# Differential attention and a Hadamard FFN on one core: the third input block transposed by VectorE through DRAM, FFN weights in 256-byte runs, transform levels in other steps

## The chip, the core and the metric

The kernel runs on one NeuronCore of a Trainium2 chip. The core has a matrix engine (TensorE, PE in the profile; PEld is its weight load), VectorE (DVE), ScalarE (ACT), GpSimd (POOL), an engine that only issues transfers (SyncE, SP), and 16 DMA engines. Data lie in SBUF (128 partitions), in PSUM (the accumulators that TensorE writes) and in DRAM. Each engine works through its own instructions in order and waits at semaphores for the others. The metric is the device time of one execution in microseconds (us), lower is better.

## The reference

The input x has 2048 tokens of 256 numbers, all in float32. Two layers follow, each with its residual:

```python
x = x + _layernorm(attention(_layernorm(x)))
x = x + _layernorm(ffn(_layernorm(x)))

# attention: 8 pairs of query heads (D = 128), 4 groups of key/value pairs
p = softmax(q1 @ k1.T) - lam * softmax(q2 @ k2.T)    # causal, 2048 x 2048 for each pair
o = p @ v                                             # v is 256 wide
o = o * rsqrt(mean(o * o) + EPS) * subln_w * (1.0 - LAMBDA_INIT)
return o @ out_w.T + out_b

# ffn: fwht is the normalised Walsh-Hadamard transform over the last dimension
x = fwht(x * SU_ug) / SCALE
x = silu(x @ W_gate.T * s_gate) * (x @ W_up.T * s_up)
x = fwht(x * SU_dp) / SCALE
x = x @ W_down.T * s_down
```

## The kernel before, in words

**Units and steps.** The attention of a group g (4 groups) is cut into units. `Unit(g, i, subs)` stands for row block i of 128 tokens: the first eight blocks are one unit each (both halves of 64 rows, "short"), the last eight two units (one half each, "long"). A program written out by hand runs one step per unit: in step s the scores and exponentials of unit s, the combination of the two softmaxes of unit s-1 (`combine`, L332 for the factor `cf` and L337 for the sum) with its transposition (`turn`, L360, and the way through DRAM, L362 and L372), and `values` (L388) of unit s-3. `inverse` on GpSimd (L415 to L418) and `turn_out` (L434) bring a finished block's output to `project_out` (L455). Group 0 has steps 0 to 23, group 1 has steps 24 to 47, with the long units first. The table of `put` calls adds other work to a step: ahead of it (`before`), behind the first half of its scores (`mid`, `between`) or at its end (`after`). An engine's order of instructions is the order in which this program is written.

**The scores.** A unit's two score products go to PSUM tiles of 1024 columns, of which three rotate (`ps_s`, shared with the projections). VectorE empties them (L279, and L290 for the last 64 columns under the mask) into `e` and finds the minimum; ScalarE takes exponentials in place (L305).

**A transposition without TensorE.** VectorE's stream transpose turns each 32x32 block of a tile. The tile is then stored to DRAM and loaded back by four transfers, one for each band of 32 partitions, which puts the blocks in their places. With pairs of rows laid beside each other the runs are 64 numbers (256 bytes), else 32 (128 bytes).

**The input.** x comes in four blocks of 512 tokens (`xt`, three buffers of a pool `xin`). Each is normalised (`norm_in`, L88 to L103) and transposed to `xnT`, from which queries, keys (`project_heads`, L176, emptied by L195 on ScalarE and L197 on VectorE) and values (`project_values`, L205, emptied by L212) are computed. Block 0 is transposed in halves by TensorE (L503), blocks 1 and 2 by TensorE (`turn_in`, L517, two copies L518 on ScalarE and VectorE), block 3 by VectorE and DRAM (`turn_by_dram`: L523, store L525, four loads L529), with a buffer `xw` of its own.

**The FFN weights.** The transforms are folded into the weights while attention runs. For each of up, gate and down, `load_weights` (L581, a DMA issued by GpSimd) brings 128 x 2048 numbers to a buffer `t0`; down is scaled on ScalarE (L589); `transform` (L612) does one level of the transform with eight GpSimd instructions of 128x256, alternating between the buffers `t0` and `t1`: 8 levels for up and gate, 10 for down. `turn_weights` (L629, four VectorE transposes; L632, one store) puts them to DRAM. Much later, in the last group, `arrive_weights` (L644, four loads for each matrix, issued by SyncE) brings them back in runs of 128 bytes.

**The steps of this work.** The tuple beside "up", "gate" and "down" in the `put` table names a step for each level; loading is at the end of `begin_at`, and the four weight transposes follow the last level by one to three steps (one `after`, one `mid`, one `after`, one `mid`). GpSimd meets the levels of a step behind that step's `inverse` and `pad` (L324, zeros behind the last column). In step 29 it also issues the load of the output weights of group 1 (`load_wo`, L149), which must wait until TensorE has used those of group 0.

Of the kernel before, what the change touches and what calls it, by code (L numbers as in the profile page):

```python
# [10 lines left out]
F32 = mybir.dt.float32  # L11
# [5 lines left out]
P = 128  # L17
# [10 lines left out]
NFC = INTER // P  # L28
# [20 lines left out]
def kernel(  # L49
# [14 lines left out]
    nc = tc.nc  # L64
# [48 lines left out]
    with ExitStack() as actx:  # L113
# [5 lines left out]
        dram = actx.enter_context(tc.tile_pool(name="dram", bufs=4, space=bass.MemoryType.DRAM))  # L119
# [349 lines left out]
        xin = pstack.enter_context(tc.tile_pool(name="xin", bufs=3, side="right"))  # L469
        xsm = pstack.enter_context(tc.tile_pool(name="xsm", bufs=2, side="right"))  # L470
        xts = []
        for b in range(NB):
            xt = xin.tile([P, 4, HID], F32, tag="xt", name=f"xt_{b}")
# [45 lines left out]

        def turn_by_dram(b):  # L520

            xw = xin.tile([P, 2 * 512], F32, tag="xw", name=f"xw_{b}", bufs=1)
            nc.vector.transpose(xw.rearrange("p (c t f) -> p t c f", c=2, t=4), xts[b].rearrange("p t (c f) -> p t c f", c=2))  # L523
            dr = dram.tile([8, 4, 32, 4, 32], F32, tag="dx", name=f"dx_{b}", bufs=2)
            nc.sync.dma_start(  # L525
                dr.rearrange("g b k a w -> (b k) g (a w)"), xw.rearrange("p (g w) -> p g w", g=8)
            )
            for a in range(4):
                nc.sync.dma_start(  # L529
                    xnT[ts(a, 32), b].rearrange("k c (n w) -> k (c n) w", w=32),  # L530
                    dr[:, :, :, a, :].rearrange("g b k w -> k (g b) w"),
                )
# [37 lines left out]
        ffn = {}  # L570
# [7 lines left out]
        def load_weights(which):  # L578
            w = {"up": wup, "gate": wgate, "down": wdown}[which]
            ffn["mixed"] = ffn["tmp"].tile([P, 2 * INTER], F32, tag="t0", name=f"raw_{which}")  # L580
            nc.gpsimd.dma_start(  # L581
                ffn["mixed"].rearrange("p (c f) -> p c f", f=w.shape[1]),
                w.rearrange("(c p) f -> p c f", p=P),
            )

        def scale_down():
# [27 lines left out]

        def turn_weights(which, part):

            w = ffn["mixed"]
            if part == 0:
                ffn["turned"] = ffn["tmp"].tile([P, 2 * INTER], F32, tag="t1", name=f"x_{which}")
            xw = ffn["turned"]  # L620

            order = "p (c f w) -> p f c w"
            src = w.rearrange(order, c=2, f=NFC) if which == "down" else w.rearrange(order, c=NFC, f=2)
            dst = xw.rearrange("p (f c w) -> p f c w", f=src.shape[1], c=src.shape[2])
            if which == "down":
                cut = lambda v: v[:, ts(part, 2)]
            else:
                cut = lambda v: v[:, :, ts(part, 2)]
            nc.vector.transpose(cut(dst), cut(src))  # L629
            if part == 3:  # L630
                ffn["dr", which] = dram.tile([16, 4, 32, 4, 32], F32, tag="dw", name=f"dw_{which}")
                nc.sync.dma_start(  # L632
                    ffn["dr", which].rearrange("g b k a w -> (b k) g (a w)"),
                    xw.rearrange("p (g w) -> p g w", g=16),
                )

        def room_for_weights():
# [4 lines left out]

        def arrive_weights(which, a):
            nc.sync.dma_start(  # L644
                ffn[which][ts(a, 32)].rearrange("k (n w) -> k n w", w=32),
                ffn["dr", which][:, :, :, a, :].rearrange("g b k w -> k (g b) w"),
            )

# [164 lines left out]
        before, mid, between, after = {}, {}, {}, {}  # L813

        def put(where, step, f, *args, **kw):
            where.setdefault(step, []).append(lambda: f(*args, **kw))
# [20 lines left out]
        put(before, 0, project_heads, 0, 1, 1, both=False, n=256)  # L837
        put(mid, 0, turn_in, 1)
        put(mid, 0, norm_in, 2)
        put(mid, 0, project_heads, 0, 1, 2, both=False, n=256)  # L840
        put(mid, 0, project_values, 0, 1)
        put(mid, 0, project_heads, 0, 1, 1, both=True)
        put(mid, 0, lambdas)
        put(between, 0, project_heads, 0, 1, 2, both=False)
        put(before, 1, turn_in, 2)
        put(mid, 1, norm_in, 3)
        put(mid, 1, project_heads, 0, 1, 0, both=True)
        put(mid, 1, turn_by_dram, 3)
        put(mid, 1, project_heads, 0, 2, 0, both=False)
        put(mid, 1, project_heads, 0, 2, 2, both=True)  # L850
# [33 lines left out]
        put(after, 5, open_fold)  # L884
        for which, begin_at, steps in (
            ("up", 5, range(7, 15)),
            ("gate", 17, range(18, 26)),
            ("down", 28, (29, 30, 31, 32, 33, 33, 34, 35, 36, 37)),
        ):
            put(after, begin_at, load_weights, which)  # L890
            if which == "down":
                put(after, begin_at + 1, scale_down)
            for n, step in enumerate(steps):
                put(after, step, transform, which, n)
            for part in range(4):
                put((after, mid)[part % 2], steps[-1] + 1 + (part + 1) // 2, turn_weights, which, part)
        put(after, 40, lambda: ffn["tmp_stack"].close())
        put(after, first + 2, room_for_weights)
        for j, which in enumerate(("up", "gate", "down")):
            for a in range(4):  # L900
                put(after, first + 2 + 4 * j + a, arrive_weights, which, a)
            put(after, first + 6 + 4 * j, sign_weights, which)
# [22 lines left out]
        for step in range(len(units) + LAG + 4):  # L925
            for f in before.get(step, ()):
                f()
            new, mixed = at(step), at(step - 1)
# [104 lines left out]
```

## Time and profile before

| | us |
|---|---|
| median of 3 runs | 1442.96 |
| lowest and highest of them | 1442.91, 1444.27 |
| the profiled execution's own time | 1442.67 |
| its span, first to last instruction | 1440.9 |
| TensorE busy | 1431.5 |
| VectorE busy | 1039.4 |
| ScalarE busy | 508.3 |
| GpSimd busy | 358.7 |

The profile records one execution. Its page gives the busy time of each engine, the span in 40 slices, the DMA queues, the chain of work that ended last and the costliest groups of instructions. Other views of the same trace give the waits of one engine (what it waited for, us in total, times, longest) and a timeline (start in us, duration in us, engine, line, operation, output and input, shape, count; in square brackets the idle time just before and what ended it). Neighbouring instructions of one kind are merged in the timeline. The ends of matmuls are modelled and overlap the next start, so gaps of TensorE are counted from start to start. In a row such as `wup<-dw_up SPq DMA_DIRECT2D x4, 256.0 KB, 7.2` the last number is the median time from the issue of a transfer to its landing.

### The profile page before, as it was taken

How to read it: one execution, taken by the hardware profiler on the slowest of the kernel's cores; microseconds unless marked ns; L12 is line 12 of the kernel's file. 1: busy time of each engine (PE TensorE's matmuls, PEld its weight loads, DVE VectorE, ACT ScalarE, POOL GpSimd, SP SyncE). 2: the span in 40 equal slices, each digit the busy share in tenths (PEclk: the TensorE clock that was granted, in tenths of full speed). 3: DMA queues.
4: the chain of work that ended last, by engine and by line, in shares of the span. 5: the costliest groups of instructions: out<-in, count | busy, mean ns of one | idle time of the engine just before them, and what ended most of it. 6: DMA issues, size and time to landing. Idle time of an engine off the chain costs nothing.

```text
span 1440.9 us, 17707 instructions
## 1 busy us (share of the span) xinstructions
PE 1431.5 (99%) x5444; PEld 1038.5 (72%) x5444; DVE 1039.4 (72%) x2453; ACT 508.3 (35%) x1115; POOL 358.7 (25%) x683
## 2 busy tenths in 40 slices
PE   9999999999999999999999999999999999999998
PEld 7567767656766776776677776675777777888887
DVE  6588897847666888644868779545877799766774
ACT  3453433323123334333433334323424445531111
POOL 2037724632007851011111111111111121121110
PEclk9999999999999999999999999999999999999999
DMA  3379889956487788832788887731999999732110
GB/s 118 73 169 197 198 181 208 191 88 139 94 186 153 163 185 196 166 85 66 153 186 177 173 202 162 134 81 52 206 204 192 192 193 191 166 96 81 52 52 22
DMA packets 511725, 209.75 MB, mean 146 GB/s; under 512 B 404144, under 2 KB 509616, under 8 KB 511632
## 3 DMA queue, kind: packets, MB, share of 16 engines
q1 hardware_dynamic: 508016, 199.42, 66.0%
q0 software_dynamic: 2480, 8.26, 2.2%
q10 hardware_dynamic: 1136, 0.95, 0.2%
q8 instruction: 44, 0.72, 0.2%
q14 instruction: 49, 0.40, 0.1%
HBM read 110.52 MB, written 98.04 MB: 145 GB/s over the span
## 4 chain that ended last, share of the span: by engine, by line
PE 96%; DVE 2%; DMA 1%; issue 0%; POOL 0%; SPq 0%; ACT 0%; POOLq 0%; DVEq 0%
PE po L388 32%; PE sc L264 31%; PE pp L176 11%; PE gu L713 8%; PE pout L455 8%; PE pd L748 4%; PE pv L205 4%; DMA dr<-e 0%; DMA vb<-in_vbias 0%; DVE e L279 0%; PE warm L488 0%; DMA pt<-dr 0%; DVE e L337 0%; DVE e L360 0%; DVE cf L332 0%
## 5 line engine op out<-in xcount | busy, mean ns | idle before, releaser
L388 PE MATMUL po<-v,pt 128*128 128x256 f32 x2176 | 488.2, 379 | 0.4 <-DMA pt<-dr 0.4
L264 PE MATMUL sc<-k,q 128*128 128x512 f32 (+7 forms) x1280 | 478.6, 519 | 2.0 <-DVE last L290 0.9
L388 PEld LDWEIGHTS po<-v,pt 128*128 128x128 f32 x2176 | 425.6, 196 | 60.3 <-issue 11.2
L264 PEld LDWEIGHTS sc<-k,q 128*128 128x128 f32 x1280 | 237.6, 190 | 215.2 <-issue 182.3
L305 ACT ACTIVATE e<-e,last 128x192 f32<-128x192 f32 (+28 forms) x256 | 299.6, 1171 | 223.9 <-DVE last L290 206.2
L279 DVE TENSOR_SCALAR_CACHE_REDUCE e<-sc 128x1024 f32<-128x1024 f32 (+15 forms) x248 | 231.1, 932 | 171.0 <-PE sc L264 169.7
L401 ACT COPY osb<-po 128x256 f32<-128x256 f32 (+1 forms) x96 | 42.5, 443 | 463.7 <-PE po L388 463.7
L415 POOL TENSOR_TENSOR u<-ss,ed 128x1 f32<-128x1 f32 (+1 forms) x96 | 18.3, 191 | 749.4 <-ACT po L404 749.2
L337 DVE SCALAR_TENSOR_TENSOR e<-e,cf,e 128x64 f32<-128x64 f32 (+31 forms) x128 | 173.5, 1376 | 3.4
L360 DVE STREAM_TRANSPOSE e<-e 128x768 f32<-128x768 f32 (+7 forms) x192 | 172.4, 937 | 4.8
L176 PE MATMUL pp<-xnT,wq 128*128 128x512 f32 (+1 forms) x408 | 170.6, 568 | 0.2 <-DVE xnT L504 0.2
L176 PEld LDWEIGHTS pp<-xnT,wq 128*128 128x128 f32 x408 | 77.0, 190 | 78.3 <-issue 74.8
L455 PE MATMUL pout<-wo,oT 128*128 128x256 f32 x512 | 121.0, 379 | 0.0
L279 DVE TENSOR_SCALAR_CACHE_REDUCE e<-sc,mx 128x320 f32<-128x320 f32 (+13 forms) x128 | 97.2, 759 | 21.6 <-PE sc L264 7.8
L455 PEld LDWEIGHTS pout<-wo,oT 128*128 128x128 f32 x512 | 97.2, 190 | 13.1 <-issue 0.3
L290 DVE CUSTOM_DVE_ANT_0 e<-sc,mask,mx 128x64 f32<-128x64 f32 x248 | 70.4, 284 | 8.9
L726 ACT ACTIVATE hT<-gu,colv 128x256 f32<-128x256 f32 x64 | 26.8, 470 | 120.5 <-PE gu L713 120.5
L713 PE MATMUL gu<-fxnT,wgate 128*128 128x256 f32 x256 | 65.8, 379 | 0.0
L713 PE MATMUL gu<-fxnT,wup 128*128 128x256 f32 x256 | 65.7, 379 | 0.0
L418 POOL TENSOR_SCALAR osb<-osb,f 128x256 f32<-128x256 f32 x128 | 61.3, 479 | 12.4
L416 POOL TENSOR_TENSOR f<-u,mhalf 128x1 f32<-128x1 f32 (+1 forms) x96 | 58.4, 608 | 7.5
L732 DVE SCALAR_TENSOR_TENSOR hT<-gu,colv,hT 128x256 f32<-128x256 f32 x64 | 30.6, 478 | 40.5 <-ACT hT L726 40.5
(101 smaller groups left out, 1107.1 us busy)
## 6 DMA issues: line engine op xcount, KB each, us to landing
dr<-e SPq DMA_DIRECT2D x20, 1024.0 KB, 4.7
pt<-dr SPq DMA_DIRECT2D x80, 256.0 KB, 5.7
dr<-e SPq DMA_DIRECT2D x20, 896.0 KB, 4.4
pt<-dr SPq DMA_DIRECT2D x80, 224.0 KB, 5.1
do<-xo SPq DMA_DIRECT2D x64, 256.0 KB, 4.0
oT<-do SPq DMA_DIRECT2D x256, 64.0 KB, 2.6
dr<-e SPq DMA_DIRECT2D x20, 768.0 KB, 4.5
pt<-dr SPq DMA_DIRECT2D x80, 192.0 KB, 4.4
```

Of the source, the lines that this page charges most:

```text
L176: nc.tensor.matmul(pp[:, 512 * h : 512 * h + n], lhsT=wq[:, c, ts(j, P)], rhs=xnT[:, xb, c, lo : lo + n], start=(c == 0), stop=(c == 1),)
L264: nc.tensor.matmul(sc[:, 512 * k : 512 * k + ww], lhsT=qT[m][:, u.i, u.subs[a]].rearrange("d p q -> d (p q)"), rhs=kT[m][:, at + lo : at + ...
L279: nc.vector.tensor_scalar(dst, src, 1.0, best, ALU.mult, ALU.min, accum_out=u.mx[:, k0, c : c + 1],)
L290: nc.vector.tensor_tensor_reduce(e[:, L - 64 : L], sc[:, tail : tail + 64], mask, 1.0, best, ALU.add, ALU.min, accum_out=u.last[:, k0 : k0 ...
L305: nc.scalar.activation(e, e, AF.Exp, bias=u.last[:, 2 * a + m : 2 * a + m + 1], scale=-1.0, accum_out=u.d[:, a, m : m + 1],)
L337: nc.vector.scalar_tensor_tensor(e0, e1, cf[:, a : a + 1], e0, ALU.mult, ALU.add)
L360: nc.vector.transpose(xv[:, r], ev[:, r])
L388: nc.tensor.matmul(u.po[:, ts(a, HID)], lhsT=ptv[:, g, r, :], rhs=vt[:, kc, :], start=(kc == 0), stop=(kc == u.i),)
L416: nc.gpsimd.tensor_tensor(f[:, : u.ns], w[:, : u.ns], mhalf[:, : u.ns], ALU.pow)
L418: nc.gpsimd.tensor_scalar(u.osb[:, a, :], u.osb[:, a, :], f[:, a : a + 1], 16.0, ALU.mult, ALU.mult)
L455: nc.tensor.matmul(u.pout[:, :HID], lhsT=u.oT[:, c, p, :], rhs=wos[u.g][:, p, c, :], start=(p == 0 and c == 0), stop=(p == 1 and c == 1),)
L713: nc.tensor.matmul(ps[:, ts(2 * j + n, 256)], lhsT=ffn[which][:, c, ts(fc, P)], rhs=xnT[:, c, :], start=(c == 0), stop=(c == 1),)
```

## The change

Three things are changed.

1. Block 2 of the input goes the way of block 3. `turn_in(2)`, ahead of step 1, is removed, and `turn_by_dram(2)` stands behind `norm_in(2)` in step 0. The buffers `xw` are no longer a place of their own but take the next of the three buffers of `xt`.
2. The FFN weights are loaded with pairs of rows beside each other (up and gate in four groups of two rows for each partition, down in one), so that the transposed weights are stored in DRAM with runs of 64 numbers, and arrive in runs of 256 bytes instead of 128. The scales of down are laid out to match.
3. The levels take other steps. Gate: 18 to 21, then two each in 22 and 23 (before: one each in 18 to 25). Down: loaded after step 26 (before: 28), levels in 28, 29, 29, 30, 30 and 31 to 35 (before: 29 to 32, 33, 33, 34 to 37). Their transposes and stores move with them, by two steps. Up stays.

```diff
         def turn_by_dram(b):
 
-            xw = xin.tile([P, 2 * 512], F32, tag="xw", name=f"xw_{b}", bufs=1)
+            xw = xin.tile([P, 2 * 512], F32, tag="xt", name=f"xw_{b}")
...
             nc.gpsimd.dma_start(
-                ffn["mixed"].rearrange("p (c f) -> p c f", f=w.shape[1]),
-                w.rearrange("(c p) f -> p c f", p=P),
+                ffn["mixed"].rearrange("p (g c) -> p g c", c=2 * w.shape[1]),
+                w.rearrange("(g p r) f -> p g (r f)", p=P, r=2),
             )
...
-            xw = ffn["turned"]
-
-            order = "p (c f w) -> p f c w"
-            src = w.rearrange(order, c=2, f=NFC) if which == "down" else w.rearrange(order, c=NFC, f=2)
-            dst = xw.rearrange("p (f c w) -> p f c w", f=src.shape[1], c=src.shape[2])
+
+            n, g = (NFC, 1) if which == "down" else (2, 4)
+            src = w.rearrange("p (g r n c) -> p r n g c", g=g, r=2, n=n)
+            dst = ffn["turned"].rearrange("p (n g c r) -> p r n g c", n=n, g=g, r=2)
+            r, half = part % 2, part // 2
             if which == "down":
-                cut = lambda v: v[:, ts(part, 2)]
+                dst, src = dst[:, r, ts(half, 4), 0, :], src[:, r, ts(half, 4), 0, :]
             else:
-                cut = lambda v: v[:, :, ts(part, 2)]
-            nc.vector.transpose(cut(dst), cut(src))
+                dst, src = dst[:, r, half], src[:, r, half]
+            nc.vector.transpose(dst, src)
             if part == 3:
-                ffn["dr", which] = dram.tile([16, 4, 32, 4, 32], F32, tag="dw", name=f"dw_{which}")
+                ffn["dr", which] = dram.tile([8, 4, 32, 4, 64], F32, tag="dw", name=f"dw_{which}")
                 nc.sync.dma_start(
                     ffn["dr", which].rearrange("g b k a w -> (b k) g (a w)"),
-                    xw.rearrange("p (g w) -> p g w", g=16),
+                    ffn["turned"].rearrange("p (g w) -> p g w", g=8),
                 )
...
             nc.sync.dma_start(
-                ffn[which][ts(a, 32)].rearrange("k (n w) -> k n w", w=32),
+                ffn[which][ts(a, 32)].rearrange("k (n w) -> k n w", w=64),
...
         put(mid, 0, norm_in, 2)
+        put(mid, 0, turn_by_dram, 2)
...
-        put(before, 1, turn_in, 2)
...
-            ("gate", 17, range(18, 26)),
-            ("down", 28, (29, 30, 31, 32, 33, 33, 34, 35, 36, 37)),
+            ("gate", 17, (18, 19, 20, 21, 22, 22, 23, 23)),
+            ("down", 26, (28, 29, 29, 30, 30, 31, 32, 33, 34, 35)),
...
-                    a[ff + "Wscale_dp"],
-                )
-            ],
+                )
+            ]
+            + [a[ff + "Wscale_dp"].reshape(P, 2)],
```

## The prediction, made before the result was known

> **What bounds the kernel now.** I read the page first, for its busy line and the chain of work that ended last:
>
> ```profile
> PE 1431.5 (99%) x5444; PEld 1038.5 (72%) x5444; DVE 1039.4 (72%) x2453; ACT 508.3 (35%) x1115; POOL 358.7 (25%) x683
> ...
> PE 96%; DVE 2%; DMA 1%; issue 0%; POOL 0%; SPq 0%; ACT 0%; POOLq 0%; DVEq 0%
> ```
>
> TensorE (PE) is busy for all but 9.4 us of 1440.9, and the granted clock is 9 or more in every slice. So a change that leaves the matmuls alone can win only what PE loses in gaps; the last 5 us and the first 20 hold most of those and are not touched. Next, the waits of PE alone (us in total, times, longest):
>
> ```profile
> PE warm L488 <- POOL ident masks.py:199: 1.5, 1, 1.5
> PE sc L264 <- DVE last L290: 0.9, 2, 0.7
> PE sc L264 <- DVE e L279: 0.7, 1, 0.7
> PE po L388 <- DMA pt<-dr: 0.4, 1, 0.4
> ```
>
> The first is the start. PE's timeline puts the others near 520, 1168 and 1209 us:
>
> ```profile
> 517.94 1.88 PE L264 MATMUL sc<-k,q 128*128 128x512 f32 x4
> 520.54 0.70 PE L264 MATMUL sc<-k,q 128*128 128x256 f32 x2 [0.73 <-DVE e L279]
> 521.44 2.39 PE L264 MATMUL sc<-k,q 128*128 128x512 f32 x6 [0.20 <-DVE last L290]
> ...
> 1168.61 2.40 PE L388 MATMUL po<-v,pt 128*128 128x256 f32 x10 [0.40 <-DMA pt<-dr]
> ```
>
> Matmuls overlap, so the loss is counted in starts. Pieces of 512 columns start 0.43 apart (3.43 for 8). Without a gap the two 256-wide pieces start at 517.94 + 4 x 0.43 = 519.66 and the next at 520.09; it starts at 521.44: **1.35 lost**. At 1168 the six pieces from 1166.11 take 2.10, less 0.16 overlap: 1168.05 instead of 1168.61, **0.56 lost**. At 1209, 0.74 is lost with VectorE (DVE) busy nearly throughout; nothing in the change touches it.
>
> Why is DVE late at 520? Its timeline, and GpSimd's (POOL):
>
> ```profile
> 513.72 2.05 DVE L332 SCALAR_TENSOR_TENSOR cf<-d,nlam,r 128x1 f32<-128x1 f32 x1
> 515.80 1.69 DVE L337 SCALAR_TENSOR_TENSOR e<-e,cf,e 128x1408 f32<-128x1408 f32 x1
> ```
> ```profile
> 510.24 5.51 POOL L612 TENSOR_TENSOR t_down<-t_down 128x256 f32<-128x256 f32 x8
> ```
>
> L332 writes one number per row and has a median of 0.22 us; here it takes 2.05 and ends at 515.77, when POOL's level ends (515.75). The same happens at 161.54: 1.97 us, ending within 0.03 us of a level. Other L332 beside a level take 0.23 to 0.77. The stall at 520 is this 1.83 us too much on DVE.
>
> The Trainium skill, "SBUF — State Buffer", section "SBUF: two separate sides", says a VectorE instruction with two SBUF inputs and a GpSimd one that reads SBUF exclude each other for a whole instruction. The trace agrees in kind; in length, 2.05 us is about three of POOL's 0.69 us instructions. Its rule speaks against packing levels (second rival).
>
> **The change, part by part.**
>
> *Third block.* Eight PE transposes (0.87 us in the chain), an ACT copy (0.57) and a DVE copy (0.69) go. Do the 0.87 come back? The waits in the two built programs say: the first score product of step 1 (sc_1_0_0) waits for L290 of sc_0_0_2 on DVE; the second (sc_1_0_1) for the second L195 that empties pp_1_2_512 on ACT; neither depends on the transposes.
>
> ```profile
> 31.85 0.61 PE L264 MATMUL sc<-k,q 128*128 128x128 f32 x4
> 32.29 1.04 PE L517 MATMUL pst<-ident,xt 128*128 128x128 f32 x8
> 33.17 0.82 PE L264 MATMUL sc<-k,q 128*128 128x192 f32 x4
> ```
> ```profile
> 32.05 1.26 ACT L195 ACTIVATE k<-pp,colv 128x512 f32<-128x512 f32 x2 [0.87 <-PE pp L176]
> ```
>
> PE would be free at 32.30, but L290 ends at 32.83, so the first starts at about 32.9 and would end its 0.33 by 33.22; ACT ends at 32.05 + 1.26 = 33.31, so the second starts at 33.36. Now it starts at 33.17 + 0.33 = 33.50. **Gain 0.14, not 0.87**: the transposes fill time in which PE would wait for ACT.
>
> Added: one DVE transpose of 128x1024 (1.23, as L523) after norm_in(2), which ends at 25.54. Behind it waits L212 (pv_1), ending 27.9 instead of 26.7; sc_0_0_2, which needs it, starts at 31.85, and DVE next idled 2.66 us before 29.34: hidden. The buffer it takes (xt_1's) is free when turn_in(1) ends, 19.96. SP gets one store and four loads; nothing is on its queue from 11.7 to 36.72. Block 3 took this path: transposed by 43.34, last load issued by 48.2 and landing at most 3.8 later, 8.7 in all. Now 26.7 + 8.7 = 35.4. The first reader, pp_2_0_512, comes one projection (3.43) after pp_1_0_512, which starts at 33.82 - 0.14: 37.1. Cover 1.7 us; beyond it each us is one of PE. xw_3 now takes the slot of xt_2, which the same engine has read long before: nothing.
>
> *Levels.* POOL's number of instructions stays; they move. Down's levels (8 instructions each, 5.0 to 7.1 us a level) are in steps 28, 29, 29, 30, 30, 31 to 35 instead of 29 to 32, 33, 33, 34 to 37. POOL is then free of them from about 507, so the L332 at 513.72 costs 0.22: DVE is 1.83 earlier where PE lost 1.35. In return the first transpose of down (0.69) comes in there: the evictions start 1.14 earlier instead of 1.83, that of the tile PE next needs ends at about 521.3, and PE asks for it at 520.09 + 1.72 = 521.8. **Gain 1.35.**
>
> What the packing costs: in step 29 POOL waits for wo until 435.26 as now, then two levels (12.6, as the pair at 476.94) to about 449, inverse(30) and its pad to 450; two more to 463, inverse(31) to 464.3. Who waits: turn of e_1_12_0 at 457.3 for the pad, turn_out (L434) at 468.28 for inverse(31). Cover 7 and 4 us: nothing. DVE there gets up to 0.7 per step more (L332 0.5 more, L337 0.4 more beside a level), against 2.8 to 6.8 us idle per step. Gate's pairs in steps 22 and 23 run 272.6 to 300; step 22's second level falls on L337 at 278.23: +0.4 on L337 and up to 0.3 on L332, against 0.72 idle at 286.31. Just covered. raw_down, loaded after step 26, waits for gate's last transpose as now; its scaling on ACT (2.17) falls between 402.2 and L305 at 405.60, which waits for DVE: nothing.
>
> *Weights.* The weight transposes stay 128x512 with results two elements apart, as in L360: 0.66 there, 0.69 for L629: nothing; a twofold price would be 12 x 0.69 spread over steps with idle DVE. Loads by POOL in longer runs are ahead of levels that wait anyway. dw_down (1 MB) now goes out before dr_8_0, at 545.9 on SP. A store behind dw_gate took 7.7 (426.31 to 434.00), against 5.3 for dr_8_0 now. So pt_8_0 is issued near 555 and lands near 561; its reader is at 565.2 - 1.5. Cover about 2.5: nothing, but see the rivals. The twelve arrivals are 256 KB in 1024 runs instead of 2048:
>
> ```profile
> pt<-dr SPq DMA_DIRECT2D x80, 256.0 KB, 5.7
> ...
> wup<-dw_up SPq DMA_DIRECT2D x4, 256.0 KB, 7.2
> ```
>
> pt has 256-byte runs, wup 128-byte ones: 1.5 us a transfer, in a stage (1025 to 1170) where the DMA share exceeds 1. Near 1168 the store was ready at 1154.42 and issued at 1155.54, behind a weight load that held SP for 1.25. A shorter issue and landing are worth 1 us or more on a chain that was 0.56 late; bounds 0 and 0.56. DVE is nearly full from 1161 to 1200, so PE may lean on it there: **I take 0.35**.
>
> By the Trainium skill, "DMA: Bandwidth & Descriptors", section "Specifications", transfers under 512 B are read, modified and written; 256 B would stay below that, and by it this 0.35 would be 0. The two rows above speak for a gain.
>
> *Sum.* 0.14 + 1.35 + 0.35 = 1.84. From the profiled execution's 1442.67 (span 1440.9 and 1.77 around it) that gives 1440.83; it lies 0.29 below the median, so the median becomes **1441.1**.
>
> **Rivals.**
>
> 1. *The third block arrives late (slower).* If the round trip takes as long as store and load near 1160 (1155.54 to 1168.47, 12.9 instead of 8.7), it lands at 39.6: 2.5 lost, total 1442.96 - 1.84 + 2.5 = 1443.6. It turns slower beyond 39.0. For: four loads wait for one store. Against: DMA is at 0.22 from 25 to 50 us. 7%.
> 2. *A long L332 in a packed step.* 2 of some 20 levels' L332 were long. In step 22 or 23 it would cost 1.83 - 0.72 = 1.1: 1442.2. 15%.
> 3. *dw_down delays pt_8_0.* If store and load take 2 us more each, PE waits 1.5: 1442.6. 8%.
> 4. *All gaps close* (0.87 at the start, 1.35, 0.56 and 0.74 at 1209): 3.5 gained, 1439.4. Against: the waits at 32.83 and 33.31. 10%.
> 5. *The levels' move does nothing,* because another delay of DVE takes the place of L332: 0.14 + 0.35: 1442.5. Against: the timeline from 510.59 to 521.29 holds no other. 7%.
>
> **How the numbers follow.** Forecast 53%, around 1441.1 (1440.2 to 1442.0: the bounds 0 and 0.56, and 0.4 for small waits). Its range alone leaves out too much; to 1439.6 to 1443.4 come rivals 2, 3 and 5, part of 1 and 4, and about 15% stays outside. A measurement of this kernel tells about 0.2% (2.9 us) from no change: faster is below 1440.07. Rival 4 and the forecast's edge give 0.18. Slower is over 1445.85, which needs a third block over 6 us late or a stall unseen here: 0.06. The rest, 0.76, is the same.
>
> **What would show it.** Right: L332 near 514 at about 0.2 us, no PE gap between 515 and 525, a short PE wait for DVE and ACT at 32 to 33.4 us, xnT landing before 37, no wait for pt near 1168. Wrong: PE waits for xnT at 37; a new gap at 278 to 300, 436 to 470 or 560 to 566.

## The result and the profile after

| | before | changed |
|---|---|---|
| median of 21 runs, us | 1443.04 | 1441.09 |
| lowest and highest, us | 1441.82, 1445.15 | 1440.30, 1443.02 |
| the profiled execution's own time, us | 1442.67 | 1443.02 |
| its span, us | 1440.9 | 1441.2 |

The ratio is 0.9985, with a 95% interval of 0.9979 to 0.9990: 1.95 us less, between 1.4 and 3.0. The forecast was 1441.1. The profiled execution of the changed kernel is the slowest of its 21: it lost about 2 us in its first 20, for a reason that the section on hardware tells, and everything behind starts that much later. So the two traces are compared matmul by matmul: the start of each in one trace less its start in the other (the third block's eight transposes left out). This shift is level for hundreds of microseconds; where it steps, one kernel waited and the other did not.

From the page of the changed kernel, busy times and the chain of work that ended last:

```profile
PE 1431.3 (99%) x5436; PEld 1038.5 (72%) x5436; DVE 1037.9 (72%) x2453; ACT 507.7 (35%) x1114; POOL 360.9 (25%) x683
...
PE 97%; DVE 1%; DMA 1%; issue 0%; SPq 0%; ACT 0%; POOLq 0%; POOL 0%; DVEq 0%
```

Nothing has changed in kind: PE sets the time and only its gaps can be won. Its four longest waits (total, times, longest):

```profile
PE warm L488 <- POOL ident masks.py:199: 1.5, 1, 1.5
PE pp L176 <- DVE vex L91: 1.1, 1, 1.1
PE sc L264 <- DVE last L290: 0.7, 1, 0.7
PE sc L264 <- DVE e L279: 0.5, 1, 0.5
```

The wait of 0.7 for L279 at 520 and that of 0.4 for `pt` are gone. One of 0.5 for L279 is new; it lies at 35 us, where the third block's transposes stood. The shift has these steps. At 31.85 it stands at +2.03 (the start). At 33.82, behind the removed transposes, +2.01: **0.02 gained**. At 95 to 98, -0.22. At 517 to 522, **-1.43**, and +0.07 at 538 to 541: 1.36 net. At 1157 to 1160, +0.39, and at 1165 to 1169, -0.63: **0.24 gained**. From there to the end it stays at +0.17.

PE at the start, with the new wait. The first row is called the lead product here: the last scores of step 0, just ahead of the removed transposes.

```profile
33.88 0.61 PE L264 MATMUL sc<-k,q 128*128 128x128 f32 x4
35.01 0.98 PE L264 MATMUL sc<-k,q 128*128 128x192 f32 x4 [0.52 <-DVE e L279]
35.83 10.46 PE L176 MATMUL pp<-xnT,wq 128*128 128x512 f32 x24
```

From the lead product to the projection it is 35.83 - 33.88 = 1.95, against 33.82 - 31.85 = 1.97 with eight transposes between them. VectorE's and GpSimd's side of the place near 520, and PE's:

```profile
515.50 0.22 DVE L332 SCALAR_TENSOR_TENSOR cf<-d,nlam,r 128x1 f32<-128x1 f32 x1
515.76 1.68 DVE L337 SCALAR_TENSOR_TENSOR e<-e,cf,e 128x1408 f32<-128x1408 f32 x1
```
```profile
501.48 6.86 POOL L612 TENSOR_TENSOR t_down<-t_down 128x256 f32<-128x256 f32 x8
```
```profile
519.72 4.46 PE L264 MATMUL sc<-k,q 128*128 128x512 f32 x12
524.01 4.91 PE L388 MATMUL po<-v,pt 128*128 128x256 f32 x22
```

L332 takes 0.22, the last level ended at 508.34, and the twelve score products that were three pieces with two waits are one. Near 1160, where the weights arrive:

```profile
1158.13 1.99 PE L264 MATMUL sc<-k,q 128*128 128x512 f32 x6
1160.26 2.40 PE L388 MATMUL po<-v,pt 128*128 128x256 f32 x10
...
1168.86 2.33 PE L388 MATMUL po<-v,pt 128*128 128x256 f32 x10
```

The wait at 1168 is gone. A smaller one, which before did not have, stands two products earlier: six score products from 1158.13 need 1.83 (1163.52 - 1161.69 for six of the same width in before) and would let `po` start at 1159.96; it starts at 1160.26, and the step of the shift is 0.39. The view brackets no wait there, but the chain of work from 1147 to 1160 goes through the store `dr` and the load of `pt`.

### The profile page after: what moved, and what is told of

Same layout as the page of the kernel before. It is cut to its first block, busy times and chain, and to the rows that moved or that the text cites. A ratio compares the mean times of both kernels' runs of the same rounds, so it can differ in the third digit from the quotient of the medians.

```text
span 1441.2 us, 17703 instructions
## 1 busy us (share of the span) xinstructions
PE 1431.3 (99%) x5436; PEld 1038.5 (72%) x5436; DVE 1037.9 (72%) x2453; ACT 507.7 (35%) x1114; POOL 360.9 (25%) x683
## 4 chain that ended last, share of the span: by engine, by line
PE 97%; DVE 1%; DMA 1%; issue 0%; SPq 0%; ACT 0%; POOLq 0%; POOL 0%; DVEq 0%
PE po L388 32%; PE sc L264 31%; PE pp L176 12%; PE gu L715 8%; PE pout L455 8%; PE pd L750 4%; PE pv L205 4%; DMA pt<-dr 1%; DVE e L279 0%; DMA dr<-e 0%; DVE e L337 0%; DVE e L360 0%; DMA xt<-in_x 0%; SPq L372 0%; DVE xo L434 0%
## 5 line engine op out<-in xcount | busy, mean ns | idle before, releaser
L279 DVE TENSOR_SCALAR_CACHE_REDUCE e<-sc 128x1024 f32<-128x1024 f32 (+15 forms) x248 | 231.2, 932 | 170.7 <-PE sc L264 169.4
L279 DVE TENSOR_SCALAR_CACHE_REDUCE e<-sc,mx 128x320 f32<-128x320 f32 (+13 forms) x128 | 97.1, 759 | 21.6 <-PE sc L264 7.9
L290 DVE CUSTOM_DVE_ANT_0 e<-sc,mask,mx 128x64 f32<-128x64 f32 x248 | 70.4, 284 | 8.9
```

The lines of the kernel that those rows point to most:

```text
L279: nc.vector.tensor_scalar(dst, src, 1.0, best, ALU.mult, ALU.min, accum_out=u.mx[:, k0, c : c + 1],)
L290: nc.vector.tensor_tensor_reduce(e[:, L - 64 : L], sc[:, tail : tail + 64], mask, 1.0, best, ALU.add, ALU.min, accum_out=u.last[:, k0 : k0 ...
```

## The experiments

The predicted terms are of 0.1 to 1.4 us, and single runs of one kernel spread over 2 to 4. So each question is read from the trace, by the shift, and the times stand beside it: median, and the ratio to the kernel before, run beside it (medians 1443.18 to 1443.50), with its interval.

| kernel | median | ratio | interval |
|---|---|---|---|
| block_alone | 1443.80 | 1.0002 | 0.9993 to 1.0011 |
| weights_alone | 1442.38 | 0.9995 | 0.9986 to 1.0003 |
| levels_alone | 1441.80 | 0.9988 | 0.9979 to 0.9997 |
| one_level | 1441.63 | 0.9985 | 0.9976 to 0.9994 |
| fill_16 | 1442.02 | 0.9992 | 0.9982 to 1.0001 |
| other_psum | 1441.09 | 0.9985 | 0.9975 to 0.9994 |
| down_later | 1442.43 | 0.9993 | 0.9984 to 1.0003 |
| turn_late | 1441.57 | 0.9987 | 0.9977 to 0.9997 |
| no_weights | 1441.39 | 0.9989 | 0.9980 to 0.9998 |
| down_later_b | 1444.87 | 1.0013 | 1.0004 to 1.0022 |
| start_only | 1440.81 | 0.9981 | 0.9972 to 0.9990 |
| two_a_step | 1442.54 | 0.9993 | 0.9984 to 1.0002 |

**The third block: block_alone, fill_16, other_psum.** The first is the kernel before with

```diff
-            xw = xin.tile([P, 2 * 512], F32, tag="xw", name=f"xw_{b}", bufs=1)
+            xw = xin.tile([P, 2 * 512], F32, tag="xt", name=f"xw_{b}")
...
+        put(mid, 0, turn_by_dram, 2)
...
-        put(before, 1, turn_in, 2)
```

> The kernel before with the third block's new way alone; weights and levels stay as before. Theory (the eight transposes fill time in which PE waits for DVE and ACT): PE's first score product of step 1 starts about 0.15 after L290 of the second half of step 0, and pp_1_0_512 starts 0.02 to 0.14 earlier than before, counted from the lead product of step 0; time 0 to 0.15 lower, which times alone can't show. Rival (the transposes cost PE their 0.87): pp_1_0_512 0.87 earlier. Rival (the block arrives late): a wait of PE for xnT near 37.

Measured: from the lead product to pp_1_0_512 1.95, as in the changed kernel (33.92 - 31.97); 0.02 gained, no wait for `xnT` in 25 to 60 us. The rival of 0.87 falls, and so does the late block. Next the changed kernel with

```diff
+        def fill(n):
+            ps = ps_o.tile([P, 512], F32, tag="o", name="fill")
+            for k in range(n):
+                nc.tensor.transpose(ps[:, ts(k % 4, P)], ident, ident)
...
+        put(before, 1, fill, 16)
```

> The changed kernel with 16 transposes of the identity, whose result nothing reads, put on TensorE where the 8 of the third block stood. Theory (PE waits there for DVE and ACT anyway): the first 8 cost nothing, the other 8 cost 0.87; from the lead product of step 0 to pp_1_0_512 it takes 1.95 in the changed kernel and 2.75 to 2.85 here. Rival (each costs its 0.11): 3.6 to 3.7. It is also one more sample of the wait for pt between 1150 and 1175 with 256-byte runs: the changed kernel lost 0.32 there, the weights alone 1.03, three kernels with 128-byte runs 0.96, 1.34 and 1.59.

PE in fill_16:

```profile
31.87 0.61 PE L264 MATMUL sc<-k,q 128*128 128x128 f32 x4
32.31 1.91 PE L523 MATMUL fill<-ident 128*128 128x128 f32 x16
34.06 0.82 PE L264 MATMUL sc<-k,q 128*128 128x192 f32 x4
34.71 10.46 PE L176 MATMUL pp<-xnT,wq 128*128 128x512 f32 x24
```

34.71 - 31.87 = 2.84. With none it is 1.95, with 8 (before) it is 1.97, with 16 it is 2.84: the first eight are free, the next eight cost their 0.87. That is the theory's shape, and it is shown. What the wait is for, other_psum tells; it is the changed kernel with

```diff
-                    sc = ps_s.tile([P, 1024], F32, tag="sc", name=f"sc_{u.n}_{k0}_{c}")
+                    sc = (
+                        ps_o.tile([P, 512], F32, tag="o", name=f"sc_{u.n}_{k0}_{c}")
+                        if (u.g, u.i, half) == (0, 1, 0)
+                        else ps_s.tile([P, 1024], F32, tag="sc", name=f"sc_{u.n}_{k0}_{c}")
+                    )
```

> The changed kernel with the two first score products of step 1 in the PSUM pool that the transposes used, instead of the one whose three buffers are still being emptied. Theory (what held PE at 34 us was buffers, not matmuls): no wait of PE ahead of these products; pp_1_0_512 0.5 to 0.8 earlier after the lead product than in the changed kernel. Rival (PE would wait all the same, for the next buffer): under 0.2 gained. One more sample of the wait for pt between 1150 and 1175.

```profile
32.03 1.26 PE L268 MATMUL sc<-k,q 128*128 128x128 f32 x8
33.17 10.54 PE L176 MATMUL pp<-xnT,wq 128*128 128x512 f32 x24
```

The eight score products of both steps run as one piece, and the projection follows 1.14 after the lead instead of 1.95. The shift to the changed kernel steps by -0.74 here (0.07 of the difference is lost again between the projection's first two matmuls). So most of the transposes' 0.87 could be had, but not by taking the transposes away alone: it also takes a free PSUM buffer for the scores that follow. This kernel does both; the buffer with the transposes still in place was not run.

**The levels: levels_alone, one_level.** The edits, each to the kernel before:

```diff
 levels_alone
-            ("gate", 17, range(18, 26)),
-            ("down", 28, (29, 30, 31, 32, 33, 33, 34, 35, 36, 37)),
+            ("gate", 17, (18, 19, 20, 21, 22, 22, 23, 23)),
+            ("down", 26, (28, 29, 29, 30, 30, 31, 32, 33, 34, 35)),
 one_level
-            ("down", 28, (29, 30, 31, 32, 33, 33, 34, 35, 36, 37)),
+            ("down", 28, (29, 30, 31, 32, 33, 33, 34, 35, 37, 37)),
```

> The kernel before with the levels' new steps alone. Theory (L332 at 513.7 waits for POOL's level): that L332 takes 0.22, no PE gap from 515 to 525, 1.35 to 1.43 gained there and in the time, no new gap at 272 to 300 or 436 to 470. Rival (the step only moves which instruction is late): a gap of 0.5 or more stays between 515 and 540, gain under 0.9.

> The kernel before with one level of down moved: the ninth goes from step 36 to step 37, the nine others stay. It takes GpSimd away from beside L332 at 513.7 and nothing else. Theory: L332 there at 0.2 to 0.3 instead of 2.05 and the 1.35 at 520 gone, as with all levels moved; a new long L332 one step later at most. Rival (the gap came from the sum of down's transposes and levels at this place): the gap stays over 0.7.

In levels_alone the shift steps by -1.43 at 517 to 522 and by +0.07 at 539, and stands still from 98 to 517, so the pairs of levels cost nothing. In one_level it steps by the same -1.43 though nine of down's ten levels stay where they were. VectorE, GpSimd and PE in one_level:

```profile
513.67 0.22 DVE L332 SCALAR_TENSOR_TENSOR cf<-d,nlam,r 128x1 f32<-128x1 f32 x1
...
522.02 0.51 DVE L332 SCALAR_TENSOR_TENSOR cf<-d,nlam,r 128x1 f32<-128x1 f32 x1
```
```profile
520.42 12.32 POOL L612 TENSOR_TENSOR t_down<-t_down 128x256 f32<-128x256 f32 x16
```
```profile
517.88 4.46 PE L264 MATMUL sc<-k,q 128*128 128x512 f32 x12
522.18 4.91 PE L388 MATMUL po<-v,pt 128*128 128x256 f32 x22
```

With GpSimd idle at 513.67 the same L332 takes 0.22; one step on it runs beside two levels back to back and takes 0.51, and PE does not feel that. One level beside one instruction was the whole stall. Counted against the changed kernel, four traces with the old steps (before, block_alone, weights_alone, down_later_b) lose 1.36 or 1.37 between 500 and 545, and every trace with new ones loses 0.0.

**The weights: weights_alone and no_weights.** weights_alone is the kernel before with `load_weights`, `turn_weights`, `arrive_weights` and the order of Wscale_dp as in the changed kernel; no_weights is the changed kernel with these four as before (one line of each edit is shown):

```diff
 weights_alone
-                ffn[which][ts(a, 32)].rearrange("k (n w) -> k n w", w=32),
+                ffn[which][ts(a, 32)].rearrange("k (n w) -> k n w", w=64),
 no_weights
-                ffn[which][ts(a, 32)].rearrange("k (n w) -> k n w", w=64),
+                ffn[which][ts(a, 32)].rearrange("k (n w) -> k n w", w=32),
```

> The kernel before with the weights in 256-byte runs alone. Forecast's theory: the twelve loads of 256 KB land in 5.7 instead of 6.4 to 7.2 us, and PE's loss of 0.56 near 1168 shrinks by 0.2 to 0.56. What the changed kernel's trace suggests: the loads land in 6.0 to 7.1 as there, a wait for pt stays in the stretch from 1155 to 1170, 0.25 shorter or the same. By the Trainium skill, DMA: Bandwidth & Descriptors, Specifications, both lengths are under 512 B and nothing is gained. A wait of 0.2 us at 96 (pout) goes if the load of raw_up in longer runs is its cause, and stays if it was chance.

> The changed kernel with the weights back in 128-byte runs (third block and levels as changed). From 1150 to 1180 five executions with 256-byte runs have lost 0, 0, 0.2, 0.3 and 1.0 us so far, four with 128-byte runs 0.6, 1.0, 1.3 and 1.6. Theory (the shorter runs make pt late there): 0.9 to 1.6 lost, time 0.4 to 1 above the changed kernel's 1441.1. Rival (chance; by the Trainium skill, DMA: Bandwidth & Descriptors, Specifications, both lengths pay the same): 0 to 0.4 lost, time 1441.1.

Both missed the theory: weights_alone lost 1.10, more than before's 0.63, and no_weights 0.26, as its rival said. What PE loses between 1148 and 1182 differs from trace to trace. It is counted by the shift against the four traces that lose least there (turn_late, down_later, down_later_b and two_a_step, which agree to 0.01), which makes it up to 0.1 more than the figures in the expectations:

| runs of the weight loads | lost by PE, us | mean |
|---|---|---|
| 128 bytes (before, block_alone, levels_alone, one_level, no_weights) | 0.63, 1.42, 1.66, 1.03, 0.26 | 1.00 |
| 256 bytes (weights_alone, changed, fill_16, other_psum, turn_late, start_only) | 1.10, 0.39, 0.35, 0.07, 0.00, 0.62 | 0.42 |

The means speak for the theory, the ranges overlap, and no_weights, the one kernel that differs from the changed one in nothing else, lost less than it (0.26) and has a median 0.3 above, well within the intervals. Whether the run length made PE faster **is not settled**. The landings say little for it. This is the changed kernel's list of transfers:

```profile
wup<-dw_up SPq DMA_DIRECT2D x4, 256.0 KB, 7.1
wgate<-dw_gate SPq DMA_DIRECT2D x4, 256.0 KB, 6.5
wdown<-dw_down SPq DMA_DIRECT2D x4, 256.0 KB, 6.0
```

In before they were 7.2, 6.7 and 6.4. By the Trainium skill, "DMA: Bandwidth & Descriptors", section "Specifications", transfers under 512 bytes are read, modified and written. Both lengths lie under that, and the section names no difference between them; the landings, 0.1 to 0.4 us shorter, nearly agree. One thing did change in every trace: what SyncE issues right behind a load of wdown. Here before, then the changed kernel:

```profile
1154.19 1.25 SPq L644 DMA_DIRECT2D wdown<-dw_down  x1
1155.54 3.03 SPq L362 DMA_DIRECT2D dr<-e  x1
```
```profile
1154.80 1.29 SPq L646 DMA_DIRECT2D wdown<-dw_down  x1
1156.19 1.45 SPq L362 DMA_DIRECT2D dr<-e  x1
```

The reader is to compare the second rows: the same store holds SyncE for 3.03 or 1.45 us, and for 0.38 where no such load is ahead. Over the last three loads of wdown it is 2.34 to 4.46 in the five traces with 128-byte runs (15 values) and 0.92 to 1.54 in the six with 256 (18 values), without overlap. So half as many runs do free SyncE sooner there, by 1.6 us in these two rows. It hardly moves `pt`, though: the loads behind this store are issued at 1162.45 in before and at 1162.70 in the changed kernel, which runs 0.42 later there.

**Where the weight loads stand: down_later, down_later_b, two_a_step.** The first two are the changed kernel and the kernel before with

```diff
-                put(after, first + 2 + 4 * j + a, arrive_weights, which, a)
-            put(after, first + 6 + 4 * j, sign_weights, which)
+                put(after, first + 2 + 4 * j + a + 4 * (j == 2), arrive_weights, which, a)
+            put(after, first + 6 + 4 * j + 4 * (j == 2), sign_weights, which)
```

> The changed kernel with the four loads of wdown each four steps later, so that none stands on SP's queue between those of pt from 1131 to 1166. Theory (the loss near 1160 to 1170 is pt held up by the weight loads): no wait of PE for pt there, under 0.1 lost from 1150 to 1180, 0.3 less than in the changed kernel's trace and up to 1.5 less than in the worst seen. Rival (the stage is limited by the transfers of e and pt themselves): a wait of 0.3 or more stays.

> The kernel before, 128-byte runs, with the four loads of wdown each four steps later. Theory (the loss is pt standing behind weight loads on SP): under 0.1 lost from 1150 to 1180 though the runs are short, 0.56 less than in the trace of before; the later wait near 1246 (1.7 with 256-byte runs, a transposition that waits for the FFN's store) may come here too. Rival (short runs hurt wherever they are read, or the stage is limited by e and pt): 0.4 or more stays there, or comes between 1170 and 1210 where the loads now are.

Both lose 0.00 between 1148 and 1182 by the count above, with 256-byte and with 128-byte runs. But both lose more later: 1.73 and 2.21 at 1246. In down_later VectorE and PE show

```profile
1240.50 0.77 DVE L434 STREAM_TRANSPOSE xo<-osb 128x256 f32<-128x256 f32 x2 [5.57 <-DMA df<-xf]
```
```profile
1246.22 0.59 PE L264 MATMUL sc<-k,q 128*128 128x192 f32 x2 [0.58 <-DVE hT L735]
```

The two names `xo` and `xf` are one buffer (one tag, bufs=1). SyncE issues the store `df` from it at 1236.10, behind loads of `pt` and `oT` that had to wait for their own stores (5.8 and 3.3 us), 0.42 later than in the changed kernel although PE is 1.9 us further on here; until it has landed, VectorE idles 5.57 us (3.38 in the changed kernel, which costs PE nothing), and then PE waits for VectorE. For the third kernel the loads come two a step, in start_only (below):

```diff
-                put(after, first + 2 + 4 * j + a, arrive_weights, which, a)
-            put(after, first + 6 + 4 * j, sign_weights, which)
+                put(after, first + 2 + (4 * j + a) // 2, arrive_weights, which, a)
+            put(after, first + 5 + 2 * j, sign_weights, which)
```

> The kernel start_only with two loads of weights in a step instead of one, so that the last is issued six steps earlier, near 1090, and none stands among the loads of pt from 1131 to 1166. Theory (weight loads on SP make pt late near 1160): under 0.1 lost from 1150 to 1180 and, if the stage at 1030 to 1090 has the room that one load a step suggests, none lost there; 0 to 0.3 faster than start_only. Rival (twice the loads a step make pt late earlier): a wait of 0.5 or more between 1030 and 1100.

```profile
1104.99 2.84 PE L392 MATMUL po<-v,pt 128*128 128x256 f32 x12 [0.43 <-DMA pt<-dr]
...
1118.36 2.84 PE L392 MATMUL po<-v,pt 128*128 128x256 f32 x12 [0.95 <-DMA pt<-dr]
```

Again 0.00 from 1148 to 1182, and 1.87 lost at 1105 and 1117 instead: the rival's wait for `pt` comes, a little later than the 1030 to 1100 that it named. The three kernels without weight loads among the loads of `pt` lose nothing near 1160, with either run length, and the eleven with them lose up to 1.66, nine of them 0.26 or more. That points to these loads as the cause; with one trace of each kernel it is no more than that. Neither of the two other places tried was free, and one a step was the better choice.

**The wait at 1209: turn_late.** The changed kernel with

```diff
-            late = mixed and mixed.ns == 2 and (0 < mixed.g < NG - 1 or mixed.g == 0 and mixed.i in (3, 4))
+            late = mixed and mixed.ns == 2 and (0 < mixed.g < NG - 1 or mixed.g == 0 and mixed.i in (3, 4) or mixed.g == 3 and mixed.i == 6)
```

> The changed kernel with combine's successor of one unit (group 3, block 6: its transposition and way through DRAM) put behind the second half of the next scores. Theory (PE loses 0.74 at 1209 because DVE transposes ahead of emptying the scores): the wait for L290 at 1209 goes, 0.6 to 0.74 gained, nothing lost later since pt is read three steps on. Rival (DVE is full here and the wait only moves): a wait of 0.3 or more within the next 20 us. One more sample of the wait for pt between 1150 and 1175.

```profile
1209.33 1.32 PE L264 MATMUL sc<-k,q 128*128 128x512 f32 x4 [0.83 <-DVE last L290]
```

The rival holds: the wait goes from the first of these products to the last, 0.09 is gained, and 0.99 is lost at 1246 by the wait for `df` just told. VectorE is busy for 48.5 of the 51 us from 1161 to 1212 in the changed kernel; what is put behind one product is in the way of the next.

**The start: start_only.** The changed kernel with other_psum's edit and

```diff
+        def keep_busy():
+            ps = ps_s.tile([P, 1024], F32, tag="sc", name="busy")
+            for k in range(6):
+                nc.tensor.matmul(ps[:, :P], lhsT=ident, rhs=ident, start=True, stop=True)
...
+        put(before, 0, keep_busy)
```

> The changed kernel with the two score products of step 1 in the other PSUM pool, and six matmuls of the identity ahead of the first projection, which nothing reads. Theory (a wait of 1.05 us or more at 7 us is followed by 3.41 us of half clock, one of 0.94 or less is not): no half clock, the first projection takes 3.7, and no runs 2 us above the rest; 0.74 gained at 34 us as before; median 1440.0 to 1440.5. Rival (the halved clock doesn't hang on PE's idleness): it is still seen, or the runs still fall in two groups 2 us apart.

The first projection takes 3.69, no half clock is seen, and the eleven runs lie between 1440.60 and 1441.07, where the changed kernel's 21 lie between 1440.30 and 1443.02. The median of 1440.81 is above the 1440.0 to 1440.5 expected: the six matmuls (12 instructions in the trace) run until 7.95, while the projection could start at 7.16 in the trace of before. It has the lowest median of all, but its interval overlaps the changed kernel's, so it is not shown to be faster than that.

## Why the prediction was right, step by step

The time was right, 1441.09 for 1441.1, and the step that carried most of it was right in place, cause and size. Of the two small steps one was mis-sized and one rested on a number that is not a constant, so that the total fits to 0.01 us is luck.

- **Levels, 1.35: right.** 1.43 at 520 less 0.07 at 539. L332 went from 2.05 to 0.22 as said. one_level shows that this one meeting was all of it, and that nothing else of the move earned anything. The packing cost nothing: L332 beside a packed pair took at most 0.54 (441.98), beside a single one of the moved levels at most 0.73 (470.90), and PE waited for neither.
- **Third block, 0.14: mechanism right, size wrong.** It measured 0.02. PE did wait for VectorE and then for ScalarE, as the step said. From the changed kernel, what each of the two score products waits for, and the second product's first matmul:

```profile
34.57 0.28 DVE L290 CUSTOM_DVE_ANT_0 e<-sc,mask,mx 128x64 f32<-128x64 f32 x1
34.09 1.27 ACT L195 ACTIVATE k<-pp,colv 128x512 f32<-128x512 f32 x2 [0.87 <-PE pp L176]
35.41 0.42 PE L264 MATMUL sc<-k,q 128*128 128x192 f32 x1
```

L290 ends at 34.86 and the first product starts at 35.01 (the view names the L279 behind it, which ends only then). That is 0.15 where the step took 0.07, and it costs nothing, because the second product has to wait for ScalarE's end at 35.35 anyway. It starts at 35.41, which is 33.38 on the clock of before (2.03 earlier) and close to the 33.36 of the step: 0.12 gained. What the step had wrong is what follows. It let the product run as in before, where its two matmuls and the projection start at 33.50, 33.66 and 33.82. Behind the wait they start at 35.41, 35.67 and 35.83: 0.42 instead of 0.32, and 0.10 of the gain is gone. Why the first matmul behind a wait takes longer, no run here shows.

The cover for the new path was 1.7, as said. The four loads of `xnT`:

```profile
L529 SPq DMA_DIRECT2D xnT<-dx x4: 335/554/964, 32.1 to 33.7; - x4
DMA to landing us min/median/max: 2.7/3.6/3.9
```

The last is issued at 33.7 and none lands later than 3.9 after its issue, so all are there by 37.6; their reader starts at 35.83 + 3.43 = 39.26.

- **Weights, 0.35: unsettled.** In the two traces it is 0.24. The step took the 0.56 lost near 1168 in one trace as the kernel's loss; five traces with 128-byte runs lose 0.26 to 1.66 there. It also took 5.7 as the new landing, from `pt`, which has the same bytes and run length; it became 6.0 to 7.1. Only the shorter issue came as said (1.45 for 3.03).
- **The rest of the baseline.** Before's trace lost 0.2 at 96, where `pout` waited; weights_alone lost most of it too, the twelve other kernels did not, down_later_b among them, which is the kernel before up to 1160. It was chance, and the prediction did not see it.

In the two traces the terms sum to 0.02 + 1.36 + 0.24 = 1.62, against 1.84 forecast and 1.95 (1.4 to 3.0) in the medians; the 0.33 between 1.62 and 1.95 is within that interval and not accounted for.

Of the rivals, the late third block did not come (no wait for `xnT`), nor a long L332 in a packed step, nor a late pt_8_0: dw_down went out at 544.94, the store behind it held SyncE 1.15, and the view shows no wait of PE from 500 to 600. "All gaps close" came true in part: that at 520 did, those at 1209 (0.74) and at the start stayed. "The levels' move does nothing" is refuted by levels_alone (0.9979 to 0.9997) as by its trace.

## What to carry to other kernels

Work that fills a wait is free, and taking it away alone gains next to nothing; before counting removed matmuls as gain, ask what the next one waits for (here a PSUM buffer), and free that as well. A loss read from one trace is one sample: where it hangs on transfers that compete, take several traces before pricing its removal, while a loss that comes from an order of instructions repeats to 0.01 us. And when one big move earns something, look for the one meeting of two instructions that paid: here a single level put one step later gave all that thirteen in new places gave.

## What the hardware showed that was not expected

**Half clock after a short idle stretch at the start.** The changed kernel's profiled execution, three stretches (us, then busy time of PE, PEld, DVE, ACT and POOL, the granted clock, DMA share, GB/s), and its first projection:

```profile
5.00:8.50 3.50, 2.05 (x12) 1.42 (x11) 2.65 (x11) 1.06 (x2) 1.27 (x3) 1.00 0.92 287
8.50:11.90 3.40, 3.40 (x9) 2.66 (x8) 0.85 (x3) 0.54 (x2) 2.92 (x7) 0.50 0.72 242
11.90:15.30 3.40, 3.40 (x19) 2.99 (x18) 1.59 (x6) 1.40 (x4) 1.27 (x2) 1.00 0.82 138
```
```profile
8.00 5.38 PE L176 MATMUL pp<-xnT,wq 128*128 128x256 f32 x16 [1.12 <-DVE vex L91]
```

PE waits 1.12 us, starts at 8.00, and has half its clock for 3.41 us; the sixteen matmuls take 5.38 where 3.69 to 3.72 is usual. weights_alone shows the same after a wait of 1.05. Waits of 0.94 (block_alone) and 1.00 (down_later_b) at the same place were not followed by it. The length of the wait is not all that tells these traces apart: in the first 3.41 us at full clock PE was busy for 1.96 us in the changed kernel (5.09 to 8.50) and 1.87 in weights_alone (4.30 to 7.71), and for 2.14 (block_alone) to 3.41 in the twelve others. Which of the two decides is open. The Trainium skill, "TensorE: Matmul & The Clock Gate", section "Why this matters for your kernels", asks for no gap above about 3 us; here one of 1.05 to 1.12, with PE busy 2.05 of the 3.5 us around it in the changed kernel, was followed by half the clock, so the measurement differs from it. Both executions are the slowest of their kernels' runs. Of the changed kernel's 21 runs five lie at 1442.29 to 1443.02 and the others at 1441.58 or below; with PE kept busy (start_only) none of 11 stands apart like that. That every such run had the half clock is not shown, since only profiled executions tell the clock; and two_a_step, with the same matmuls at the start, spreads from 1441.12 to 1443.90 again, so the times alone do not settle it.

**The issue of a transfer pays for the one ahead.** A store that SyncE issues in 0.38 us takes 0.92 to 1.54 behind a load of 1024 runs and 2.34 to 4.46 behind one of 2048, over the last three loads of wdown. The price appears in the row of the next transfer, not in the load's own (1.29 and 1.25 in the rows above). Elsewhere the two ranges meet: behind a load of wup at 1069.8 in the changed kernel the store took 3.11.
